# Attention layer and graph convolution on one core: the bias stores moved behind the row products, norms two rows at a time, one copy moved between engines, one start a unit later

## The chip, the cores and the metric

The kernel runs on one core of a Trainium2 chip. The metric is the device time of one execution in microseconds (us), the median of the runs shown. The core has five engines with a queue of instructions each: TensorE (PE in the profile) multiplies matrices, VectorE (DVE) and ScalarE (ACT) do elementwise work and can read PSUM, where products accumulate, GpSimd (POOL) does elementwise work on SBUF, and SyncE (SP) issues transfers. POOL issues transfers too.

## The reference

All is float32; x is 4096 x 512 and adj is 4096 x 4096. Layer 0 is an attention whose scores have adj added twice, with a residual and a norm; layer 1 is a graph convolution with a residual and a norm.

```python
def _layernorm(x, axis=-1, eps=1e-5):
    m = jnp.mean(x, axis=axis, keepdims=True)
    v = jnp.var(x, axis=axis, keepdims=True)
    return (x - m) / jnp.sqrt(v + eps)

# layer 0: _L0_gnn_ref(x, adj, adj, Wq, bq, Wk, bk, Wv, bv)
q = x @ Wq.T + bq
k = x @ Wk.T + bk
v = x @ Wv.T + bv
a = q @ k.T * scale + spatial_encoding + edge_encoding   # both are adj
attn = jax.nn.softmax(a, axis=-1)
x = _layernorm(x + attn @ v)

# layer 1
h = jax.nn.relu(adj @ (x @ W1) + b1)       # W1: 512 x 128
out = adj @ (h @ W2) + b2                  # W2: 128 x 512
x = _layernorm(x + out)
```

## The kernel before

**Groups and units.** The 4096 query rows are cut into 8 groups of 512. A group's scores are made in 16 units of two key tiles each. Score products, sums of probabilities times x ("P x", line 488) and most other large products are cut by a scheme of seven half-size products in place of eight, in the order 1, 2, 6, 7, 5, 4, 3 (`ORDER`). A unit has seven slots, and in each slot PE does one half of a score product (line 351) and DVE reads one (line 364).

**What runs beside the scores.** While PE makes the scores of group g+1, the probabilities of group g are finished: DVE subtracts the row maximum (`shift`, line 394), ACT takes the exponential (line 398), POOL adds the row sums (`sums`, line 407) and two combinations of quarters (`px_t2`, lines 434 and 435), DVE forms further combinations (`px_t34`, line 441, and `px_t1`, line 446), and PE multiplies by x. The table `PREP` gives the unit and the slots in which each of the 16 pairs of a group is prepared; group 0 has its own first two entries (`PREP_FIRST`) and the last group its own first seven (`PREP_LAST`). P x is done in blocks of key pairs (0-2, 2-4, 4-8, 8-12, 12-16), in each block the seven products, and `px_read` takes a finished product from PSUM into `ot`: in the first block the products 1, 6, 7 and 3 are copied by ACT (line 459), all others are added by DVE (line 461). The items of P x lie in a list that is worked off between the score products, at a rate that spreads it over the units given: for group 0 from the third unit after its scores on (`work[s1 + 2]`, 15 units), for later groups from the second on (16 units). In the last group there are no further scores: the row work of group 6 is followed by three times as much P x in each gap, and six products of the next stage (line 936) are mixed in.

**Row work.** When P x of a group is done, its rows are multiplied by Wv (`rows_out_fast`, line 602, for groups 0 to 5; `rows_out`, line 563, for 6 and 7), x is added, DVE takes mean and variance of each row tile of 128 rows (lines 536 and 538), POOL turns them into a factor and a shift in three small instructions (lines 544, 545, 547), and ACT applies them (`rows_norm`, line 551). This gives x1. `add_b2` then has POOL add the bias b2 (line 631) and issue the store of x1 + b2 to DRAM (line 633), to be read in the last stage only. The buffers of these sums (`xb`) come from the ring of eight (tag `sa`) into which SP loads the keys of the scores (lines 252 and 257). PE transposes x1 (`project`, line 639), ACT copies the result (line 641), PE multiplies it by W1 (`project2`, line 648) and DVE copies that (line 651). `row_items` is the list that sets the order; `w(n)` stands for n items of P x between two of its steps:

```python
        def norm(r):
            return [item(0, rows_norm, g, r), item(0, add_b2, g, r)]
```

So in the kernel before the sum and the store of a row stand directly behind its norm.

**Order.** Each engine works its instructions in the order in which the program emits them; the program emits them slot by slot. There is no other scheduler. The pool `form` of the first stage is closed at unit 18, and memory that it held is used again, among others by the first `ot` (`OT[0]`) and by the fourth buffer for x (`load_x(3)`, which waits in SP's queue). That memory is free once the store `u_d<-uo` of the first stage has been read out; POOL computes the last `uo` (line 206) and issues that store (line 196).

**After the groups** come the two products with adj (line 936 and the stages behind it) and the last norm.

Of the kernel before, what the change touches and what calls it, by code (L numbers as in the profile page):

```python
# [11 lines left out]
F32 = mybir.dt.float32  # L12
AF = mybir.ActivationFunctionType
ALU = mybir.AluOpType
# [4 lines left out]
P = 128  # L19
# [5 lines left out]
def tile_graph_attention_then_gcn(  # L25
# [51 lines left out]
    nc = tc.nc  # L77
# [4 lines left out]
    NG = N // W  # L82
    NP = NT // 2
# [14 lines left out]
    half_t = const.tile([P, 1], F32, name="half_t")  # L98
# [26 lines left out]
    small = att.enter_context(tc.tile_pool(name="small", bufs=4, side="right"))  # L125
# [30 lines left out]
    UT, UO, XTS, SA, S, XN, CB, MB, MACC, LACC, O, OT, RL, XR, T = ({} for _ in range(15))  # L156
# [293 lines left out]
    def px_read(g, first, k):  # L450

        letter = "PX" if k in (1, 6, 5, 3) else "PY"
        ps = T[letter].rearrange("p (f i) -> p f i", f=2)
        f, i = {1: (0, 0), 2: (0, 0), 6: (1, 0), 7: (1, 1), 5: (1, 1), 4: (1, 0), 3: (0, 1)}[k]
        to = OT[g][:, 2 * f : 2 * f + 2, ts(i, HW)]

        def go():
            if first and k in (1, 6, 7, 3):
                nc.scalar.copy(to, ps)  # L459
            else:  # L460
                nc.vector.tensor_tensor(to, ps, to, ALU.add)  # L461

        px_reads.append((letter, go))

    def read_px(letters=("PX", "PY")):
        for one in list(px_reads):
            if one[0] in letters:
                px_reads.remove(one)
                one[1]()
# [64 lines left out]
    def stats_of(pool, r):  # L534
        stats = pool.tile([P, nc.vector.BN_STATS_DIM], F32, tag="stats", name="stats")
        nc.vector.bn_stats(stats, r)
        mv = pool.tile([P, nc.vector.BN_AGGR_DIM], F32, tag="mv", name="mv")
        nc.vector.bn_aggr(mv, stats)
        return mv

    def norm_stats(pool, r, eps=EPS):
        mv = stats_of(pool, r)
        rstd = pool.tile([P, 1], F32, tag="rstd", name="rstd")
        nc.gpsimd.tensor_scalar(rstd, mv[:, 1:2], eps, None, ALU.add)
        nc.gpsimd.tensor_tensor(rstd, rstd, half_t, ALU.pow)
        shift = pool.tile([P, 1], F32, tag="shift", name="shift")
        nc.gpsimd.tensor_scalar(shift, mv[:, 0:1], rstd, -1.0, ALU.mult, ALU.mult)
        return shift, rstd

# [21 lines left out]
    def rows_out_fast(g, k, j):  # L571

        ot = OT[g].rearrange("p (f c) (h i) -> p f h c i", f=2, h=2)
        a11, a12, a21, a22 = (ot[:, f, h] for h in range(2) for f in range(2))
        tt = nc.vector.tensor_tensor

        def read(k):
            ps = T["VX" if k in (1, 6, 5, 3) else "VY"].rearrange("p (j o) -> p j o", j=2)  # L580
            h, i = QUARTER[k]
            to = XR[g][:, 2 * h : 2 * h + 2, ts(i, HW)]
            tt(to, ps, to, ALU.add)

        def stats(*rs):
            for r in rs:
                T["norm", g, r] = norm_stats(small, XR[g][:, r, :], RL[g][:, r : r + 1])

        if (k, j) == (1, 0):
            read_px()  # L590
            T["s3"] = rowp.tile([P, 2, HW], F32, tag="x1t", name=f"s3_{g}")
            tt(T["s3"], a11, a21, ALU.subtract)
            tt(a21, a21, a22, ALU.add)
        if j == 0 and k in (1, 2, 7):
            if k != 1 and m_tags[0] == T["v tag"]:
                m_tags.reverse()
            T["VX" if k == 1 else "VY"] = mbank(f"v{g}_{k}")
            if k == 1:
                T["v tag"] = m_tags[-1]
        lhs = {1: a11, 2: a12, 6: a11, 7: T["s3"], 5: a21, 4: a22, 3: a12}[k]  # L600
        for c in range(2):
            nc.tensor.matmul(  # L602
                T["VX" if k in (1, 6, 5, 3) else "VY"][:, ts(j, HW)],
                lhs[:, c, ts(j, P)],
                WV[OPERANDS[k][1]][:, c, :],
                start=k in (1, 2, 7) and j == 0 and c == 0,
                stop=c == 1,
                skip_group_check=True,
            )
        n = ORDER.index(k)  # L610
        if j == 0 and n:
            read(ORDER[n - 1])
            if k == 2:
                tt(a11, a21, a11, ALU.subtract)
            if k == 6:
                tt(a12, a12, a11, ALU.subtract)
            if k == 3:
                stats(2, 3)
        if (k, j) == (3, 1):
            T["last", g] = lambda: (read(3), stats(0, 1))  # L620

    def rows_last(g):
        T.pop(("last", g))()
# [29 lines left out]
    def row_items(g, between):  # L653

        def item(us, f, *args):
            return us, lambda: f(*args)

        def out(r):  # L660
            return [item(0.86, rows_out, g, r, c) for c in range(ND)]

        def norm(r):
            return [item(0, rows_norm, g, r), item(0, add_b2, g, r)]

        def pro(r):
            return [item(0.44, project, g, r)]

        def pro2(r):
            return [item(0.9, project2, g, r)]  # L670

        w = between
        if g in FAST_V:
            return [
                *(item(0.86, rows_out_fast, g, k, j) for k in ORDER for j in range(2)),
                *w(1), item(0, rows_last, g), *norm(2), *norm(3), *w(2), *pro(2), *w(2), *pro(3),
                *w(1), *norm(0), *w(1), *pro2(2), *norm(1), *w(2), *pro(0), *w(2), *pro2(3), *w(2),
                *pro(1), *w(2), *pro2(0), *w(4), *pro2(1),
            ]
        return [  # L680
            *out(0), *out(1), *norm(0), *out(2), *norm(1), *out(3), *norm(2), *w(2), *pro(0),
            *norm(3), *w(2), *pro(1), *w(2), *pro2(0), *w(2), *pro(2), *w(2), *pro2(1), *w(2),
            *pro(3), *w(2), *pro2(2), *w(4), *pro2(3),
        ]


    with tc.tile_pool(name="wqk", bufs=1) as wp:
# [52 lines left out]
        for w_t, w_n in ((wq_t, wq_n), (wk_t, wk_n)):  # L740
            for o in range(ND):
                ps = bank("o", f"psw{o}", 4)
# [7 lines left out]
        for a in range(ND):  # L750
            ps = bank("o", f"psm{a}", 4)
# [42 lines left out]
    work = {}  # L794
# [149 lines left out]
    def strassen(n, beside, done=()):  # L944
# [52 lines left out]
    PREP = [  # L997
        (1, LATE), (2, EARLY), (2, LATE), (3, MID), (4, EARLY), (4, LATE), (5, EARLY), (5, LATE),
        (6, MID), (7, MID), (8, EARLY), (8, LATE), (9, MID), (10, MID), (11, MID), (12, MID),
    ]  # L1000

    PREP_FIRST = [(1, (2, 3, 4)), (1, (4, 5, 6)), *PREP[2:]]
    PREP_LAST = [
        (1, (2, 2, 3)), (1, (3, 4, 4)), (1, (5, 6, 6)), (2, EARLY), (2, LATE), (3, LATE), (4, MID),
        *PREP[7:],
# [2 lines left out]
    for n in range(NG * NG * len(ORDER)):  # L1008
        (g, d), k = divmod(n // len(ORDER), NG), ORDER[n % len(ORDER)]
        if g:  # L1010
            unit, place = divmod(2 * (n - 5), len(ORDER))
            at(unit, place, load_s, g, d, k)

    for g in range(NG):
        s0 = g * NP
        s1 = s0 + NP
        if g:
            for n, k in enumerate(ORDER):
                at(s0 - 2 + (2 * n + 1) // 7, (2 * n + 1) % 7, load_operand, g, k)
            at(s0 - 2 - (g == 1), 1, add_c0, g)  # L1020
            at(s0 - 2 - (g == 1), 3, row_consts, g)
        for q in range(NP):
            d, j = divmod(q, 2)
            if (g or d) and j == 0:
                early = 2 + (g == 1 and d == 0)
                at(s0 + q - early, 4, begin_scores, g, d)
                at(s0 + q - early, 5, add_scores, g, d)
            for h in range(2):
                n = 1 + 3 * (2 * j + h) if d < NP // 2 - 1 else 2 * j + h
                at(s0 + 2 * d + 2 + n // 7, n % 7, new_max, g, q, h)  # L1030
            unit, (n0, n1, n2) = {0: PREP_FIRST, NG - 1: PREP_LAST}.get(g, PREP)[q]
            at(s1 + unit, n0, shift, g, q, 0)
            at(s1 + unit, n1, shift, g, q, 1)
            at(s1 + unit, n1, exps, g, q)
            at(s1 + unit, n2, sums, g, q)
            at(s1 + unit, n2, px_t2, g, q)
        at(s1, 5, turn_max, g)
        at(s1 + 1, 1, spread_max, g)
        if g < NG - 1:
            at(s1 + 13, 4, row_sums, g)  # L1040
        at(s1 + 14, 0, load_rows, g)
        at(s1 + 15, 0, add_bv, g)
        px = px_items(g)
        if g == NG - 1:
            for n, (u, k) in enumerate(spare):
                px.insert((8, 14, 20, 26, 90, 150)[n], (0.86, lambda u=u, k=k: product(u, k)))
        if g:
            px.reverse()
            by = 3 if g == NG - 1 else 1
            items = row_items(g - 1, lambda n: [px.pop() for _ in range(n * by)])  # L1050
            work[s1 + 1] = NP, items + px[::-1]
        else:
            work[s1 + 2] = NP - 1, px

    for n in range(3):
        at(NP + 1, 2 + n, load_x, n)
# [9 lines left out]
    for unit in range(last_unit):  # L1066
# [30 lines left out]
        for n in range(len(ORDER)):  # L1097
            run(unit, n)
            g, place = divmod(unit * len(ORDER) + n, NP * len(ORDER))
# [19 lines left out]
    g = NG - 1  # L1119
# [26 lines left out]
    hp, _, yp, rowp, small = pools  # L1146
# [144 lines left out]
```

## Time and profile before

| what | value |
|---|---|
| median of 3 runs | 2352.41 us (2351.85 to 2352.57) |
| the profiled execution's own time | 2352.5 us |
| its span in the trace | 2350.7 us |
| mean granted clock of PE | 0.996 |
| PE busy | 2303.9 us (98%) |
| DVE busy | 1626.5 us (69%) |
| POOL busy | 1013.6 us (43%) |
| ACT busy | 401.4 us (17%) |

The span runs from the first to the last instruction; the execution's time has 1.8 us more around it. The stages follow one another in the span: preparation and the scores of group 0 up to about 251 us, then one group in some 217 us, the last scores at 1745 us, P x of the last group to 1900 us, the products with adj from there to about 2265 us, and the tail. A busy share is a mean over these stages, so the views by window tell more than the totals.

### The profile page before, as it was taken

The numbers are of one execution on the slowest core, as the hardware profiler recorded it, in microseconds if no ns is written. First come the engines' busy times: TensorE is split into PE (matmuls) and PEld (weight loads), VectorE is DVE, ScalarE is ACT, GpSimd is POOL, SyncE is SP. The second block draws the span as 40 slices with busy tenths as digits, with TensorE's granted clock in tenths as the row PEclk, the third lists the DMA queues.
The fourth block names the chain that finished last, engine by engine and source line by source line (L and its number), as shares of the span: only waits on it lengthen the run. The fifth ranks groups of instructions, "written<-read, shape, count | busy, mean of one in ns | idle before, by whom it ended". The sixth has DMA issues, their size and how long they took to land.

```text
span 2350.7 us, 28200 instructions
## 1 busy us (share of the span) xinstructions
PE 2303.9 (98%) x10518; PEld 1726.2 (73%) x10518; DVE 1626.5 (69%) x2266; ACT 401.4 (17%) x421; POOL 1013.6 (43%) x1023
## 2 busy tenths in 40 slices
PE   9999999999999999999999999999998999999998
PEld 5666788878888888888888888888885843333456
DVE  4556476686668766866776686668656777888864
ACT  2111211131112112211311221121102100000012
POOL 1566464184327424641752284236428840011043
PEclk9999999999999999999999999999998999999999
DMA  5889787757758784777577577857663658999996
GB/s 159 268 274 312 217 226 204 206 159 200 217 152 212 198 237 118 206 201 224 147 207 214 159 199 199 227 129 218 185 198 100 205 205 313 334 348 370 352 383 223
DMA packets 276887, 523.28 MB, mean 223 GB/s; under 512 B 19152, under 2 KB 126416, under 8 KB 275856
## 3 DMA queue, kind: packets, MB, share of 16 engines
q1 hardware_dynamic: 229040, 406.12, 51.6%
q0 software_dynamic: 42176, 105.39, 20.5%
q10 hardware_dynamic: 5536, 9.97, 1.2%
q8 instruction: 84, 1.38, 0.2%
q14 instruction: 51, 0.42, 0.1%
HBM read 473.44 MB, written 46.40 MB: 221 GB/s over the span
## 4 chain that ended last, share of the span: by engine, by line
PE 85%; DVE 7%; POOL 4%; DMA 2%; issue 1%; ACT 0%; POOLq 0%; SPq 0%; DVEq 0%; ACTq 0%
PE p L488 29%; PE X L351 16%; PE b L936 15%; PE Y L351 12%; PE psu L171 4%; DVE s L394 3%; PE v L602 3%; PE acce L1236 2%; PE ops L1190 1%; DVE s L364 1%; POOL lacc L407 1%; DVE macc L373 1%; DVE s L441 1%; PE tps L648 1%; PE x L563 1%
## 5 line engine op out<-in xcount | busy, mean ns | idle before, releaser
L488 PE MATMUL p<-s,xn 128*128 128x256 f32 x3584 | 901.7, 381 | 24.9 <-ACT ot L459 6.9
L488 PEld LDWEIGHTS p<-s,xn 128*128 128x128 f32 x3584 | 678.7, 191 | 134.3 <-DVE s L446 8.7
L351 PE MATMUL X<-ut,sa 128*128 128x256 f32 x1984 | 514.1, 382 | 3.7 <-DVE s L364 3.7
L351 PEld LDWEIGHTS X<-ut,sa 128*128 128x128 f32 x1984 | 371.1, 190 | 88.1 <-issue 25.1
L407 POOL TENSOR_TENSOR lacc<-lacc,s 128x512 f32<-128x512 f32 x240 | 345.5, 1440 | 185.1 <-ACT s L398 175.3
L364 DVE TENSOR_TENSOR s<-X,s 128x512 f32<-128x512 f32 x256 | 176.3, 689 | 300.0 <-PE X L351 295.9
L351 PE MATMUL Y<-ut,sa 128*128 128x256 f32 x1408 | 361.1, 379 | 1.1 <-DMA sa<-in_xT_dram 1.1
L351 PEld LDWEIGHTS Y<-ut,sa 128*128 128x128 f32 x1408 | 266.4, 190 | 47.8 <-issue 12.9
L398 ACT ACTIVATE s<-s 128x1024 f32<-128x1024 f32 x128 | 135.4, 1058 | 805.4 <-DVE s L394 805.4
L295 POOL DMA_DIRECT2D s<-in_adjT_dram x64 | 84.0, 1312 | 404.8 <-ACT s L290 401.8
L373 DVE TENSOR_TENSOR macc<-macc,s 128x512 f32<-128x512 f32 x240 | 249.6, 1040 | 1.3
L364 DVE TENSOR_TENSOR s<-Y,s 128x512 f32<-128x512 f32 x192 | 132.1, 688 | 164.4 <-PE Y L351 163.7
L394 DVE TENSOR_TENSOR s<-s,mb 128x512 f32<-128x512 f32 x256 | 236.7, 934 | 3.3 <-ACT mb L321 3.3
L461 DVE TENSOR_TENSOR ot<-p,ot 128x512 f32<-128x512 f32 x248 | 169.3, 683 | 47.4 <-PE p L488 34.0
L903 DVE TENSOR_TENSOR tt<-ck 128x1024 f32<-128x1024 f32 x112 | 138.6, 1272 | 38.9 <-PE b L936 34.5
L936 PE MATMUL b<-tt,st 128*64 128x512 f32 (+1 forms) x768 | 156.1, 541 | 0.0
L441 DVE TENSOR_TENSOR s<-s 128x512 f32<-128x512 f32 x128 | 131.8, 1050 | 0.0
L171 PE MATMUL psu<-xt,m_t 128*128 128x512 f32 x256 | 128.0, 592 | 0.0
L434 POOL TENSOR_TENSOR s<-s 128x256 f32<-128x256 f32 x128 | 123.1, 962 | 0.6
L290 ACT COPY s<-cb 128x2048 f32<-128x2048 f32 x64 | 120.8, 1888 | 0.6
L936 PEld LDWEIGHTS b<-tt,st 128*64 128x64 f32 x768 | 53.9, 137 | 87.8 <-issue 79.9
L435 POOL TENSOR_TENSOR s<-s 128x256 f32<-128x256 f32 x128 | 108.6, 848 | 10.0
(159 smaller groups left out, 1987.0 us busy)
## 6 DMA issues: line engine op xcount, KB each, us to landing
ck<-in_adjT_dram SPq DMA_DIRECT2D x128, 1024.0 KB, 7.3
s<-in_adjT_dram POOLq DMA_DIRECT2D x64, 1024.0 KB, 11.2
sa<-s_d SPq DMA_DIRECT2D x224, 256.0 KB, 4.9
xn<-in_x_dram SPq DMA_DIRECT2D x192, 256.0 KB, 3.3
xn<-xs_d SPq DMA_DIRECT2D x96, 512.0 KB, 4.5
sa<-in_xT_dram SPq DMA_DIRECT2D x168, 256.0 KB, 4.5
xn<-xs_d SPq DMA_DIRECT2D x64, 256.0 KB, 3.7
u_d<-uo POOLq DMA_DIRECT2D x7, 1792.0 KB, 7.3
```

Source lines behind the costliest of these rows:

```text
L171: nc.tensor.matmul(ps[o], m_t[:, c, ts(o, P)], XTS[b][:, c, :], start=c == 0, stop=c == ND - 1)
L351: nc.tensor.matmul(T["X" if k in (1, 6, 5, 3) else "Y"][:, ts(j, HW)], SA[g, d, a][:, c, j, :], UT[g, b][:, c, :], start=k in (1, 2, 7) an ...
L364: nc.vector.tensor_tensor(ck, ps, ck, ALU.add)
L373: nc.vector.tensor_tensor(MACC[g], MACC[g], ck[:, h, :], ALU.max)
L394: nc.vector.tensor_tensor(ck, ck, MB[g], ALU.subtract)
L398: nc.scalar.activation(ck, ck, AF.Exp, scale=2.0)
L407: nc.gpsimd.tensor_tensor(LACC[g], LACC[g], ck[:, h, :], ALU.add)
L441: nc.vector.tensor_tensor(b, b, t2, ALU.subtract)
L461: nc.vector.tensor_tensor(to, ps, to, ALU.add)
L488: nc.tensor.matmul(T["PX" if k in (1, 6, 5, 3) else "PY"][:, ts(f, HW)], XN[n][:, q - a, ts(f, P)], quarters(g, q)[{1: 0, 2: 2, 6: 1, 7: 0 ...
L903: nc.vector.tensor_tensor(t[:, :2], v[:, :, 1], v[:, 0], ALU.subtract)
L936: nc.tensor.matmul(BK[n][k][ts(half, HH)], lhs, right(u, i, half, b), start=q == 0, stop=q == NP - 1,)
```

## The change

1. `px_read` in the last group (g = 7): the four copies of the first block (products 1, 6, 7, 3) are done by DVE and not by ACT.
2. In groups 0 to 5 the two rows of a pair (2 and 3, then 0 and 1) get their factor and shift together: four POOL instructions on two columns in place of twice three on one. Groups 6 and 7 keep one row at a time.
3. `add_b2` is taken out of `norm` and becomes items of its own (`b2`), which stand at the end of `row_items`, behind the last `project2`, with P x items between them. It holds for groups 0 to 6.
4. Group 0 uses `PREP` for all its pairs, and its P x list starts one unit later and is spread over 14 units, not 15.

```diff
         def go():
             if first and k in (1, 6, 7, 3):
-                nc.scalar.copy(to, ps)
+                if g == NG - 1:
+                    nc.vector.tensor_copy(to, ps)
+                else:
+                    nc.scalar.copy(to, ps)
             else:
                 nc.vector.tensor_tensor(to, ps, to, ALU.add)
...
-        def stats(*rs):
-            for r in rs:
-                T["norm", g, r] = norm_stats(small, XR[g][:, r, :], RL[g][:, r : r + 1])
+        def stats(r):
+
+            mv = small.tile([P, 4], F32, tag="mv", name="mv2").rearrange("p (n s) -> p n s", n=2)
+            for n in range(2):
+                st = small.tile([P, nc.vector.BN_STATS_DIM], F32, tag="stats", name="stats")
+                nc.vector.bn_stats(st, XR[g][:, r + n, :])
+                nc.vector.bn_aggr(mv[:, n], st)
+            rstd = small.tile([P, 2], F32, tag="rstd", name="rstd2")
+            tt = nc.gpsimd.tensor_tensor
+            tt(rstd, mv[:, :, 1], RL[g][:, r : r + 2], ALU.add)
+            tt(rstd, rstd, half_t.to_broadcast([P, 2]), ALU.pow)
+            sh = small.tile([P, 2], F32, tag="shift", name="shift2")
+            tt(sh, mv[:, :, 0], rstd, ALU.mult)
+            nc.gpsimd.tensor_scalar(sh, sh, -1.0, None, ALU.mult)
+            for n in range(2):
+                T["norm", g, r + n] = sh[:, n : n + 1], rstd[:, n : n + 1]
...
             if k == 3:
-                stats(2, 3)
+                stats(2)
         if (k, j) == (3, 1):
-            T["last", g] = lambda: (read(3), stats(0, 1))
+            T["last", g] = lambda: (read(3), stats(0))
...
         def norm(r):
-            return [item(0, rows_norm, g, r), item(0, add_b2, g, r)]
+            return [item(0, rows_norm, g, r)]
+
+        def b2(r):
+            return [item(0, add_b2, g, r)]
...
                 *w(1), *norm(0), *w(1), *pro2(2), *norm(1), *w(2), *pro(0), *w(2), *pro2(3), *w(2),
-                *pro(1), *w(2), *pro2(0), *w(4), *pro2(1),
+                *pro(1), *w(2), *pro2(0), *w(4), *pro2(1), *w(2), *b2(2), *w(4), *b2(3), *w(4), *b2(0),
+                *w(4), *b2(1),
             ]
         return [
             *out(0), *out(1), *norm(0), *out(2), *norm(1), *out(3), *norm(2), *w(2), *pro(0),
             *norm(3), *w(2), *pro(1), *w(2), *pro2(0), *w(2), *pro(2), *w(2), *pro2(1), *w(2),
-            *pro(3), *w(2), *pro2(2), *w(4), *pro2(3),
+            *pro(3), *w(2), *pro2(2), *w(4), *pro2(3), *w(2), *b2(0), *w(4), *b2(1), *w(4), *b2(2),
+            *w(4), *b2(3),
         ]
...
-    PREP_FIRST = [(1, (2, 3, 4)), (1, (4, 5, 6)), *PREP[2:]]
...
-            unit, (n0, n1, n2) = {0: PREP_FIRST, NG - 1: PREP_LAST}.get(g, PREP)[q]
+            unit, (n0, n1, n2) = (PREP_LAST if g == NG - 1 else PREP)[q]
...
-            work[s1 + 2] = NP - 1, px
+            work[s1 + 3] = NP - 2, px
```

`PREP` begins with `(1, (3, 5, 6)), (2, (1, 2, 4))`: unit, then the slots of the two shifts, and of the row sum. The tiles of the single-row norm get two or four columns in place of one or two, of which the same ones as before are used.

More of the change, by code (lines that the diff above doesn't have):

```diff
@@ L536, in stats_of @@
         nc.vector.bn_stats(stats, r)
-        mv = pool.tile([P, nc.vector.BN_AGGR_DIM], F32, tag="mv", name="mv")
+        mv = pool.tile([P, 4], F32, tag="mv", name="mv")[:, : nc.vector.BN_AGGR_DIM]
         nc.vector.bn_aggr(mv, stats)
@@ L542, in norm_stats @@
         mv = stats_of(pool, r)
-        rstd = pool.tile([P, 1], F32, tag="rstd", name="rstd")
+        rstd = pool.tile([P, 2], F32, tag="rstd", name="rstd")[:, :1]
         nc.gpsimd.tensor_scalar(rstd, mv[:, 1:2], eps, None, ALU.add)
         nc.gpsimd.tensor_tensor(rstd, rstd, half_t, ALU.pow)
-        shift = pool.tile([P, 1], F32, tag="shift", name="shift")
+        shift = pool.tile([P, 2], F32, tag="shift", name="shift")[:, :1]
         nc.gpsimd.tensor_scalar(shift, mv[:, 0:1], rstd, -1.0, ALU.mult, ALU.mult)
```

## The prediction

> **What bounds the kernel now.** The busy table of the page comes first, then PE's waits, then windows.
>
> ```profile
> ## 1 busy us (share of the span) xinstructions
> PE 2303.9 (98%) x10518; PEld 1726.2 (73%) x10518; DVE 1626.5 (69%) x2266; ACT 401.4 (17%) x421; POOL 1013.6 (43%) x1023
> ```
>
> PE is the bound, and the change neither adds nor removes a product. So it can only fill or open holes on PE, which are worth little: 46.8 us of the span without work, and some time at half clock. The view of PE's waits says where the holes are (who waited, for whom: us in total, times, longest):
>
> ```profile
> PE p L488 <- ACT ot L459: 6.9, 3, 4.4
> PE p L488 <- POOL xb L631: 6.7, 1, 6.7
> PE p L488 <- DVE s L446: 4.3, 3, 2.0
> PE x1ps L639 <- ACT xr L551: 3.3, 6, 0.6
> ```
>
> All four are waits of P x or of a row product on something that the change moves. The windows around the two large ones (busy time of PE, PEld, DVE, ACT, POOL, then granted clock):
>
> ```profile
> 262.00:268.00 6.00, 2.96 (x8) 2.40 (x9) 1.89 (x3) 3.44 (x3) 1.75 (x3) 0.78 0.62 203
> 1770.00:1800.00 30.00, 21.14 (x81) 13.89 (x81) 15.72 (x16) 8.87 (x12) 27.16 (x32) 0.77 0.24 72
> ```
>
> In the 30 us after 1770 PE idles 8.9 us, and the clock is 0.77, while POOL is full. The timelines of ACT and POOL there (start, length, engine, line, operation; in brackets the idle time before and its releaser) explain the hole:
>
> ```profile
> 1780.36 0.81 ACT L551 ACTIVATE xr<-xr,shift,rstd 128x512 f32<-128x512 f32 x1 [6.16 <-POOL shift L547]
> 1781.08 0.56 ACT L459 COPY ot<-p 128x512 f32<-128x512 f32 x1
> ```
>
> ```profile
> 1776.77 1.26 POOL L631 TENSOR_TENSOR xb<-xr,b_t 128x512 f32<-128x512 f32 x1
> 1778.33 0.67 POOL L633 DMA_DIRECT2D x_d<-xb  x1 [0.30 <-POOL xb L631]
> 1779.08 0.23 POOL L544 TENSOR_SCALAR rstd<-mv 128x1 f32<-128x1 f32 x1
> ...
> 1780.06 0.26 POOL L547 TENSOR_SCALAR shift<-mv,rstd 128x1 f32<-128x1 f32 x1
> ```
>
> Product 6 may start at 1781.74, once the copy (L459) has read product 1. The copy stands in ACT's queue behind the norm of row 2; the norm waits for a shift that POOL makes behind a row sum and the bias sum and store of row 0. The waits view names POOL for this hole; the link to PE is ACT's copy.
>
> Earlier, ACT's first `ot` copy sits on memory:
>
> ```profile
> 264.40 0.59 ACT L459 COPY ot<-p 128x512 f32<-128x512 f32 x1 [11.72 <-DMA u_d<-uo]
> ```
>
> **What the skill says, and the trace.** (1) The Trainium skill, "TensorE: Matmul & The Clock Gate", section "What's actually happening", has PE drop to half clock after an idle window of about 3.4 us and come back after as long at work. The trace agrees: behind the holes of 4.52 and 7.08 us P x products start every 0.43 us, not every 0.216; eight such cost 1.7 us. (2) The same page, section "Architectural detail: the array is 16× 32×32, not 1× 128×128", makes ACT's queue strict first in, first out; the copy behind the norm above agrees. (3) "VectorE: DVE Perf Modes", section "Why PSUM operands drop a tier", keeps float32 from PSUM at one element a cycle; the trace has such 128x512 DVE copies at 658 ns (L1244) to 692 ns (L717) against 565 to 599 ns for ACT's L459. I use 0.66. (4) "SBUF — State Buffer", section "SBUF: two separate sides", has POOL and two-input DVE instructions lock each other out of a shared port. The trace agrees in direction: DVE L446 on 128x256 takes 1.36 us at 500.98 beside POOL's sum, where two took 1.28 at 1787.09.
>
> **The change part by part**, as PE time. Stalls below are distances between starts of PE instructions less the back-to-back distance, so a little over the waits of the views.
>
> *Group 0 a unit later.* Before, P x starts at 254.48 and needs `ot` at 260.5; the memory comes free at 264.2 (store issued at 258.20 behind 5.5 us of POOL L206). Stall 4.52, then eight products at half clock, 1.7. After, unit 18 holds scores alone, seven slots of four products at 0.215 = 6.0 us, so the copy is due at about 266.7, and 264.2 + 0.59 = 264.8 is in time. The first row sum now follows the store in POOL's queue; the store's operands come from ACT at 252.7, so it is not earlier. The next adj load (L295) moves behind it to some 266 and lands by 276, read near 275.5 to 280: 0 to 1. SP's `load_x(3)`, stuck from 246.7 to 264.3 on the same store, is asked for one unit later behind loads that then run ahead. New: in unit 18 PE outruns the reads of DVE (0.69 each, shifts 0.7 beside): 0.1 to 0.8, as the 0.95 at 253.51. The remaining P x is denser by a fifteenth: nothing, as its rate is set by PE. Sum **-5.5**, range -8 (the 1.9 of small stalls at 294 to 303 go too) to -2.
>
> *b2 behind the rows, groups 0 to 5.* Four sums of 1.3 us and four issues of 0.6 (plus 0.3 of gap), 8.4 us of POOL per group, move from slots 487.8 to 500.8 (and the like) to about 20 us later. Beside them DVE was slow: L373 2.25 us at 498.21 (mean 1.04), L394 1.53, L446 1.36, and PE waited 2.17 at 502.40 and 0.52 at 505.64; group 2 has 0.84 at 938.39 and others 0.29. Their cover gone, POOL idles there. Gain 3.5 in group 0, 0.8 in group 2: -4.3. Who is behind the moved sums? Row sums and `px_t2` of pairs 5 to 7, four to eight us later. In group 1 pair 7 ends at 746.65 and PE reads it at 775.24: 28.6 of slack; pairs 4 to 6 have 31 to 40. Their cost: nothing, or +1 of new contention. The 0.81 and 0.74 at 736.96 and 742.09 of each group stay: DVE's reads, with POOL full in both kernels. SP: the ring slots of `xb` already hold it up 86.7 us in 12 waits and 28.4 in 6, and no score product of these groups waits for a load; spread out they hold it less at a time. -4.3 to +6.
>
> *Norm pairs.* Four small POOL instructions (0.28, 0.57, 0.28, 0.28 with gaps) before two shifts, in place of three before the first and six before the second. The second row gains, but row 2 and row 0 go first: row 2's shift waits for row 3's statistics (1.0 us) and comes at 697.9 for 697 (group 1), row 0's 0.3 later. PE waits 0.72 for row 0 (six times, 3.3 in the view); I add 0.3 each in six groups: **+1.5**, from 0 to +3. With b2: **-2**, range -5 to +8.
>
> *Last group.* Four copies go from ACT to DVE: +4 x 0.66 on DVE, which has 7.48 us idle at 1781.67 for want of that copy. POOL loses two bias sums and stores (4.2 us) ahead of row 2's shift and row 3's. New order at 1774.2: DVE copies product 1 (to 1774.9), adds product 2 (0.69), L441 twice (2.1 to 3.75), L394 1.2, L446 1.28: ends 1780.8 to 1783. PE, no longer held, wants product 7 of pair 0 at 1777.9, of pair 1 at 1778.9, product 5 at 1780.5: stalls of 1 to 4, say 2.4. They replace 7.08 + 2.33 and the half clock behind them, in all 14.9 from 1781 to 1798, of which 0.9 at the mixed-in products stays. **-11.6**, range -13.5 to -5. The four b2 of group 6 now lie between pairs 8 and 12, at 1810 to 1834. POOL idles 14.2 us from 1800 to 1860 and starts that stretch 8.4 earlier, against PE earlier by 11; slack of pairs 8 to 14 is 13.7 to 31.7. Pair 15 has 2.08, but the 4.55 us of idle before pair 14 (waiting for ACT) takes up lateness first. Cost nothing; if that cover were gone, up to 6.3.
>
> Sum: 5.5 + 2 + 11.6 = 19.1 off the profiled 2352.5 (0.1 over the median), so **2333.3**.
>
> **The rivals.** *A, DVE takes the place of ACT and POOL.* Its chain from 1774 on is the next to be late; at twice what I take per link beside a full POOL, PE idles past the clock window again and the part gives 5, not 11.6; and unit 18's reads or the adj load may take back 3.5 in group 0. For it: DVE instructions at 1.9 us each at 1782; against: 7.5 us of idle on DVE beforehand. Then 19.1 - 6.6 - 3.5 = 9: 2343.5.
> *B, slower: the late b2 hold ring slots.* SP's in-order loads of the keys wait for a slot until the store lands 2.7 us after issue; SP now reaches it while POOL still has full row sums from 727 to 755 ahead. If a group's loads come 6 us past need, 7 groups cost 42: 2352.5 - 19 + 42 = 2375. It decides from 19.1 / 7 = 2.7 us per group on. For it: waits of 12.8 to 14.2 us in SP's view already; against: these stall no product, and the slots are less bunched.
> *C, nothing: within 0.2% (4.7 us, about what a measurement of this kernel can tell from no change).* Group 0's and the last group's gains are half each (9) and the pairs and new contention at 1.2 per group take 7: 2350.
>
> **How the numbers follow.** Forecast 0.60, 2326 to 2339; A 0.21, 2339 to 2347; B 0.11; C 0.08. The forecast and A are faster (0.81), C the same, B slower. Range 2325 to 2347 holds the first two. Both large holes have one named cause that the emitted order takes away; the sizes of what is late next are the doubt.
>
> **What would show it.** Right: no wait of ACT's L459 on `u_d<-uo` above 1 us, and clock 1.00 from 262 to 274; the copy in the last group a DVE line that starts near 1768 (earlier by group 0), PE's busy time over the 30 us there up from 21.1 to 26 or more; the wait on L446 near 502 gone; that on L551 still there, some 5 in all. Wrong: a hole over 3.4 us in the last group behind L441 or L446 (A), score products waiting for `sa` (B), or P x waiting for L435 by more than a microsecond.

## The result and the profile after

| | before | changed |
|---|---|---|
| median | 2351.85 us (5 runs, 2349.74 to 2352.57) | 2328.71 us (5 runs, 2328.14 to 2332.29) |
| ratio to before, 95% interval | | 0.9905 (0.9891 to 0.9919) |
| the profiled execution's own time, span | 2352.5, 2350.7 | 2332.29, 2330.5 |

The change takes off 23.1 us, 1.0%; the forecast was 19.1 (2333.3). The profiled execution of the changed kernel is the slowest of its five, 3.6 over their median. One of twelve executions of the kernel "group 0 alone" below ran at a lower clock (2426.11 us) and is left out of its figures. The busy table:

```profile
PE 2298.2 (99%) x10518; PEld 1725.5 (74%) x10518; DVE 1615.2 (69%) x2270; ACT 399.1 (17%) x417; POOL 1004.8 (43%) x999
```

PE has the same 10518 products. DVE has four instructions more and is busy 11.3 us less. PE's waits, as before (who for whom: us in total, times, longest):

```profile
PE p L491 <- DVE s L441: 5.9, 6, 1.9
...
PE X L351 <- DVE s L364: 3.9, 5, 1.0
PE p L491 <- DVE s L446: 2.6, 2, 1.7
PE x1ps L655 <- ACT xr L554: 2.3, 6, 0.4
PE Y L351 <- DVE s L364: 1.8, 1, 1.8
PE x1ps L655 <- ACT x1t L657: 1.5, 1, 1.5
```

The two rows of 6.9 and 6.7 us at the head of the list are gone. What is left is mostly DVE. A third row of before that is gone is one that the prediction does not show; it becomes important below:

```profile
PE p L488 <- POOL s L435: 3.3, 5, 0.7
```

The windows (PE, PEld, DVE, ACT, POOL busy, granted clock) that answer to those of before:

```profile
262.00:268.00 6.00, 6.00 (x30) 5.28 (x29) 3.22 (x6) 1.18 (x2) 5.84 (x7) 1.00 0.46 159
268.00:274.00 6.00, 4.67 (x22) 3.80 (x21) 6.00 (x6) 1.53 (x2) 5.84 (x6) 1.00 1.09 250
1757.00:1787.00 30.00, 27.79 (x140) 20.25 (x139) 19.96 (x31) 9.05 (x12) 27.65 (x30) 1.00 0.27 79
```

In the last group PE does 27.8 us of work in the 30 us where it did 21.1, at full clock. Around 265 us the hole is closed too, but six microseconds later PE idles 1.3 us with DVE at 6.00 of 6.00. ACT's first copy shows that the memory was no longer in the way; it waits for the product itself:

```profile
265.70 0.59 ACT L462 COPY ot<-p 128x512 f32<-128x512 f32 x1 [3.11 <-PE p L491]
```

**Where the time went.** All kernels of this study emit PE's 10518 products in one order, but for those between 254 and 450 us, where a later start of group 0 mixes the same products (of one size, but for ten) in another way. So the start of the n-th product can be compared. The table has the change of the lead against the kernel before (us, negative is won) from one of eight points to the next, at 156.9, 272.9, 438.0, 546.7, 1644.4, 1799.0, 1839.8 and 2340.7 us of the kernel before. Each row is one profiled execution, of the changed kernel its slowest.

| kernel | group 0 to 273 | 273 to 438 | rows of group 0 | rows of groups 1-5 | last group to 1799 | to 1840 | rest |
|---|---|---|---|---|---|---|---|
| changed | -5.1 | +6.3 | -4.5 | -10.5 | -11.0 | +3.4 | +0.2 |
| b2 moved alone | 0.0 | 0.0 | -4.2 | -9.7 | -2.3 | +3.3 | +0.1 |
| changed, b2 put back | -5.2 | +4.6 | -0.3 | +8.7 | -6.5 | +1.0 | +0.2 |
| pairs alone | -0.3 | 0.0 | -0.4 | +8.6 | -0.7 | 0.0 | +0.1 |
| changed, no pairs | -4.9 | +4.6 | -4.2 | -9.7 | -11.1 | +3.4 | +0.1 |
| group 0 alone | -5.2 | +4.6 | -2.1 | 0.0 | -0.2 | 0.0 | 0.0 |
| changed, group 0 as before | -1.1 | 0.0 | -4.5 | -10.5 | -11.0 | +3.5 | 0.0 |
| before, sum left out | 0.0 | 0.0 | -3.5 | -7.1 | -1.9 | +0.1 | +0.1 |
| changed, b2 of group 6 later | -4.5 | +4.6 | -4.5 | -11.0 | -11.0 | +0.1 | +3.6 |
| the same, norms reordered | -5.0 | +4.6 | -4.5 | -10.6 | -13.7 | 0.0 | +3.8 |
| the same, b2 closer together | -5.0 | +4.6 | -4.5 | -11.1 | -13.7 | 0.0 | +3.9 |
| changed, PREP_FIRST kept | -7.3 | +4.4 | -4.5 | -11.1 | -11.0 | +3.4 | +0.1 |
| combined | -7.5 | +4.4 | -4.5 | -10.6 | -13.7 | 0.0 | +3.9 |

Seven tenths of the gain lie where the prediction saw little: in the rows of groups 0 to 5, 2 us in each of five groups and 4.5 in the first. One such place, on DVE's timeline of the kernel before (start, length, engine, line):

```profile
733.96 1.17 DVE L394 TENSOR_TENSOR s<-s,mb 128x512 f32<-128x512 f32 x1
735.05 1.21 DVE L373 TENSOR_TENSOR macc<-macc,s 128x512 f32<-128x512 f32 x1
...
737.38 1.24 DVE L394 TENSOR_TENSOR s<-s,mb 128x512 f32<-128x512 f32 x1
...
739.14 2.29 DVE L441 TENSOR_TENSOR s<-s 128x512 f32<-128x512 f32 x2
```

and the same instructions in the changed kernel (the read L464 stands between them in both):

```profile
730.53 0.67 DVE L394 TENSOR_TENSOR s<-s,mb 128x512 f32<-128x512 f32 x1
731.13 1.21 DVE L373 TENSOR_TENSOR macc<-macc,s 128x512 f32<-128x512 f32 x1
...
733.47 0.68 DVE L394 TENSOR_TENSOR s<-s,mb 128x512 f32<-128x512 f32 x1
734.07 0.68 DVE L464 TENSOR_TENSOR ot<-p,ot 128x512 f32<-128x512 f32 x1
734.67 1.28 DVE L441 TENSOR_TENSOR s<-s 128x512 f32<-128x512 f32 x2
```

Two of L394 and two of L441 took 0.5 us less each. In the changed kernel DVE has idle time (0.83 us before 736.78) and PE does not wait. In the kernel before PE was held up 0.81 and 0.74 us here. The second time it waited for DVE alone. The first time two engines were late together:

```profile
736.96 0.67 PE L488 MATMUL p<-s,xn 128*128 128x256 f32 x2 [0.65 <-POOL s L435]
```

This product needs a combination that POOL makes (`px_t2`); it ended at 736.84, and DVE's read of `ot` (L461), 0.02 us later at 736.86. It is so in each of groups 1 to 5: the combination ends 0.12 us before the product starts, the read 0.10 us. In the changed kernel the combination ends 1.25 us ahead of the same product. So the sums and stores of b2 had made POOL's own work late too, and not only slowed DVE.

### The profile page after: what moved, and what is told of

It reads as the page before. It is cut to its first block, busy times and chain, and to the rows that moved or that the text cites. A ratio compares the mean times of both kernels' runs of the same rounds, so it can differ in the third digit from the quotient of the medians.

```text
span 2330.5 us, 28148 instructions
## 1 busy us (share of the span) xinstructions
PE 2298.2 (99%) x10518; PEld 1725.5 (74%) x10518; DVE 1615.2 (69%) x2270; ACT 399.1 (17%) x417; POOL 1004.8 (43%) x999
## 4 chain that ended last, share of the span: by engine, by line
PE 91%; DVE 4%; POOL 2%; issue 1%; DMA 1%; ACT 0%; POOLq 0%; SPq 0%; DVEq 0%; ACTq 0%
PE p L491 31%; PE X L351 18%; PE b L957 14%; PE Y L351 13%; PE psu L171 4%; PE v L618 3%; PE acce L1256 2%; PE ops L1210 1%; PE tps L664 1%; PE x L566 1%; DVE s L441 1%; PE x1ps L655 1%; DVE s L364 1%; PE psm L774 1%; DVE s L446 1%
## 5 line engine op out<-in xcount | busy, mean ns | idle before, releaser
L364 DVE TENSOR_TENSOR s<-X,s 128x512 f32<-128x512 f32 x256 | 176.2, 688 | 292.4 <-PE X L351 288.4
L373 DVE TENSOR_TENSOR macc<-macc,s 128x512 f32<-128x512 f32 x240 | 254.2, 1059 | 1.2
L364 DVE TENSOR_TENSOR s<-Y,s 128x512 f32<-128x512 f32 x192 | 132.0, 688 | 174.9 <-PE Y L351 174.1
L394 DVE TENSOR_TENSOR s<-s,mb 128x512 f32<-128x512 f32 x256 | 232.1, 916 | 2.5 <-ACT mb L321 2.5
L464 DVE TENSOR_TENSOR ot<-p,ot 128x512 f32<-128x512 f32 x248 | 169.0, 681 | 30.4 <-PE p L491 30.0
L441 DVE TENSOR_TENSOR s<-s 128x512 f32<-128x512 f32 x128 | 126.4, 1010 | 0.0
L435 POOL TENSOR_TENSOR s<-s 128x256 f32<-128x256 f32 x128 | 107.1, 837 | 10.0
## 6 DMA issues: line engine op xcount, KB each, us to landing
s<-in_adjT_dram POOLq DMA_DIRECT2D x64, 1024.0 KB, 11.6
```

What stands on the lines that cost most here:

```text
L364: nc.vector.tensor_tensor(ck, ps, ck, ALU.add)
L373: nc.vector.tensor_tensor(MACC[g], MACC[g], ck[:, h, :], ALU.max)
L394: nc.vector.tensor_tensor(ck, ck, MB[g], ALU.subtract)
L441: nc.vector.tensor_tensor(b, b, t2, ALU.subtract)
```

## The experiments

Theory: POOL's sums over 512 columns stretch those DVE instructions that run beside them. What the move of b2 changes is which DVE instructions these are; where P x and DVE are in step, that costs PE, and elsewhere nothing. Rivals: the norms in pairs made the gain; POOL's queue time counts (it makes POOL's own combinations late), not what its sum does to DVE; group 0's later start gained something that only the one profile hides.

**b2 moved alone.** The kernel before with the edits of `norm`, `b2` and both lists of `row_items`.

> The kernel before with the b2 items moved behind the rows' products and nothing else. Theory (POOL's sums of b2 slowed DVE in the stretch where P x and the row work wait for DVE, in every group): the gain of groups 0 to 5 in the changed kernel's trace, 15 us between the ends of group 0's P x and of group 5's rows, comes back whole here, and the 7 us hole of the last group shrinks too, since row 2's shift no longer stands behind two sums: 2351.9 - 15 - 4 = 2333, between 2329 and 2338. Rival (the norms in pairs made that gain): at most 6 us less than before, 2346 or more.

Measured: 2340.31, ratio 0.9954 (0.9939 to 0.9968), so 11.6 less than before, and above the range that I expected. Groups 0 to 5 gain 13.9, as in the changed kernel (15.0); this part of the theory holds. The last group, where I expected 4, gains nothing in the end. ACT's timeline there says why:

```profile
1764.93 0.81 ACT L551 ACTIVATE xr<-xr,shift,rstd 128x512 f32<-128x512 f32 x1 [3.96 <-POOL shift L547]
1765.65 0.56 ACT L459 COPY ot<-p 128x512 f32<-128x512 f32 x1
```

The norm still waits for POOL (row sum and `px_t2` of one pair are ahead of it), and the copy still stands behind the norm. Two sums fewer make the hole shorter by 2.3 us, and the moved sums cost 3.3 later.

**b2 put back in the changed kernel.** The reverse edit.

> The changed kernel with the b2 items put back directly behind the norms; norm pairs, DVE copies and group 0's later start stay. Theory: groups 0 to 5 lose their 15 us again, and in the last group a part of the stall comes back, as the shifts wait behind the sums though the copy does not: 2328.7 + 15 + 2 = 2346, 2341 to 2350. Rival (pairs): 2335 or less.

Measured: 2356.01, ratio 1.0021 (1.0011 to 1.0030): 10 us more than expected, and slower than the kernel before. The last group behaves as expected (-5.5 from the copies alone), but groups 1 to 5 lose 8.7 where I expected nothing won or lost. Something else in the changed kernel costs 1.7 us a group as long as b2 is in its old place; the next experiment names it.

**Pairs alone.** The kernel before with the new `stats`.

> The kernel before with the norms of groups 0 to 5 two rows at a time, nothing else. Theory from the changed kernel without its move of b2, which lost 1.8 us in each of groups 1 to 5 against the kernel before, to waits for L364, L446 and the ot read: pairs shift the sums of b2 and the row sums of POOL onto other DVE instructions, and cost while b2 is there: 2352 + 5 x 1.8 = 2361, 2358 to 2363. Rival (that loss comes from group 0's later start or the copies): 2350 to 2354.

Measured: 2360.93, ratio 1.0042 (1.0027 to 1.0056). It is the pairs. PE's waits in this kernel:

```profile
PE p L488 <- DVE s L446: 11.5, 7, 1.7
PE X L351 <- DVE s L364: 8.6, 8, 1.1
...
PE p L488 <- DVE ot L461: 4.1, 7, 0.6
```

They were 4.3, 4.6 and 1.6. With two small POOL instructions fewer for each pair of rows, POOL's first sum of b2 starts at 704.79 in group 1 where it started at 707.49, while PE is only 1.3 us ahead there. The sums and row sums now fall on the DVE instructions that P x is waiting for: by this kernel's DVE timeline, L373 takes 1.65 us at 704.97, L394 1.75 at 707.14, and the two L441 1.67 and 1.56 from 709.41 on. In the kernel before these were 0.68, 0.68, 0.68 and 1.01. Less work on POOL made the kernel 10 us slower.

**No pairs in the changed kernel.** `stats` as before.

> The changed kernel with the norms of groups 0 to 5 one row at a time again. Theory: the trace of the move of b2 alone has 9.6 us won in groups 1 to 5 against 10.5 in the changed kernel, so pairs are worth about 1 us: 2329.7, 2327 to 2332. Rival (the prediction's +1.5 for pairs): 2327 or less.

Measured: 2331.17, ratio 0.9915 (0.9900 to 0.9930), against 0.9905 for the changed kernel; the intervals overlap. In the traces the pairs win about 1 us: the rows of groups 1 to 5 have -10.5 to -11.1 in the seven kernels that have both the pairs and b2 moved, and -9.7 in the two with b2 moved and no pairs. So pairs cost 8.6 with b2 in its old place and gain about 1 with b2 moved: the sign of one edit depends on the other.

**The sum left out, the store kept.** In the kernel before:

```diff
-        xb = sap.tile(...)
-        nc.gpsimd.tensor_tensor(xb, XR[g][:, r, :], b2_t, ALU.add)
-        nc.gpsimd.dma_start(x1_d[i // 2][:, i % 2], xb)
+        nc.gpsimd.dma_start(x1_d[i // 2][:, i % 2], XR[g][:, r, :])   # g < 7
```

> The kernel before, with the sum x1 + b2 of groups 0 to 6 left out: the store of x1 itself stays where it was, so b2 is missing from the output. POOL keeps the issue (0.6 us) and loses the sum (1.3 us), as does the ring the buffers. Theory (POOL's sum reads and writes SBUF beside DVE instructions with two SBUF inputs and stretches those): most of what the move gained in groups 0 to 5 is here too, 4 us at group 0's rows and 2 in each of five others: 2351.9 - 12 = 2340, 2336 to 2343. Rival (what counts is that POOL's queue is occupied, issue and all): the 1.3 of 2.2 us each leave half, 2346 or more.

Measured: 2340.98, ratio 0.9951 (0.9936 to 0.9966). Groups 0 to 5 win 10.6 of the 13.9 that the move won, without any moved instruction. That is the theory's figure, not the rival's. But a sum left out takes 1.3 us from POOL's queue as well, so this run does not part the two: the waits for POOL's combination (L435) are gone with it too. In groups 1 to 5 they are 0.81 of some 1.9 us a group, at the place where DVE was as late; how much either would cost alone is not shown. That a part belongs to the store's queue time, or to the ring buffers that go as well, is also left open. The hole of the last group stays here too (1.9 won), now behind POOL's row sum, the two combinations and the issue of a store.

**Group 0 alone, and the changed kernel without it.** The last part of the change (`PREP` for all pairs, P x a unit later) on the kernel before, and undone in the changed one.

> The kernel before with group 0's later start and PREP for all pairs, nothing else. Theory from the trace of the changed kernel, where 4.9 us are won by 273 us and given back by 308 us to waits for DVE's L441 and L364: no gain, 2352 within 3 us. Rival (my prediction's -5.5; the loss at 301 us is of the one profiled run): 2346.

> The changed kernel with group 0 as before (PREP_FIRST, P x from the third unit). Theory: the same as the changed kernel within 3 us, 2326 to 2332, with the 4.5 us wait of the first copy on u_d back and the waits on L441 near 274 and 301 us gone. Rival: 2334 or more.

Measured: 2349.49, ratio 0.9991 (0.9982 to 1.0000); and 2329.55, ratio 0.9906 (0.9891 to 0.9921), where the changed kernel has 0.9905. Alone, group 0's later start gains some 2 us (by the interval, 0 to 4), of which the trace has 2.1 at the rows of group 0, and beside the others nothing that can be measured. The table shows the reason in every row with it: 5 us won by 273 us and 4.6 (6.3 in the changed kernel's profile) given back by 438.

**PREP_FIRST kept with the later start.** In the changed kernel the two first pairs of group 0 are prepared early again.

> The changed kernel with group 0's P x a unit later, but PREP_FIRST kept (the first two pairs prepared early). Theory: the early pairs take the DVE work of the shifts and POOL's sums out of the unit where P x starts, so part of the waits for L441 and L364 at 273 to 301 us go and 1 to 3 us of the group 0 gain stay: 2326.5, 2325 to 2329. Rival (these waits come from the density of P x alone): the same as the changed kernel, 2328.7, or more.

Measured: 2329.87 (2326.32 to 2332.52), ratio 0.9908 (0.9894 to 0.9923). Its own profile has 2.2 us more of the early gain (-7.3 to 273 us, +4.4 after), as the theory says, and so has the combined kernel below (-7.5); the median does not show it. PE's wait of 1.96 us in the unit before P x starts, at 260.96 in the changed kernel, is not there. So it came from giving up the early pairs, not from the later start. What is given back, 4.4, hardly depends on the early pairs. Most of it is waits for DVE; that the denser P x makes DVE late is likely, but no run changes the density alone.

**b2 of group 6 later.** `w(2)` ahead of the first `b2` of the list for group 6 becomes `w(13)`: 33 P x items more.

> The changed kernel with group 6's four b2 items 33 P x items later, behind product 7 of block 4-8. Theory: the 3.3 us of waits for L441 and L446 between 1808 and 1816 of the changed kernel's trace are DVE slowed beside these sums; they go: 2328.7 - 3.3 = 2325.4, 2324 to 2327. Rival (P x is so dense there that DVE is late anyway, or the later sums slow DVE elsewhere): 2328 or more.

Measured: 2330.16, ratio 0.9909 (0.9892 to 0.9925): the rival. The 3.4 us between 1799 and 1840 are gone, and 3.6 appear behind 1840. In the changed kernel these were (POOL's sum, then DVE beside it and the row sum that follows):

```profile
1805.22 1.72 POOL L647 TENSOR_TENSOR xb<-xr,b_t 128x512 f32<-128x512 f32 x1
```

```profile
1805.73 3.95 DVE L441 TENSOR_TENSOR s<-s 128x512 f32<-128x512 f32 x2
```

Two L441 in 3.95 us, where two take 1.28 undisturbed. In the later version L441 and L446 of a later block are hit: there L446 takes 3.64 us for three at 1833.20.

**Norms reordered.** On top of that, in the list for group 6, `pro(0)` stands ahead of `norm(2)` and `pro(1)` ahead of `norm(3)`.

```diff
-            *out(0), *out(1), *norm(0), *out(2), *norm(1), *out(3), *norm(2), *w(2), *pro(0),
-            *norm(3), *w(2), *pro(1), *w(2), *pro2(0), ...
+            *out(0), *out(1), *norm(0), *out(2), *norm(1), *out(3), *w(2), *pro(0), *norm(2),
+            *w(2), *pro(1), *norm(3), *w(2), *pro2(0), ...
```

> As the kernel with group 6's b2 later, and its norms of rows 2 and 3 behind the transposes of rows 0 and 1, so that ACT's copy of a transpose does not stand behind a norm that waits for POOL. Theory: the waits of 0.90 and 1.64 us for ACT's copy at 1768 and 1774 go, about 2.5 us: 2323, 2321 to 2325. Rival (the transposes of rows 2 and 3 then wait for their norms, or L441 becomes the next in line): the same as without, 2325.

Measured: 2327.16, ratio 0.9897 (0.9882 to 0.9912), 3.0 under the kernel that it is built on (the intervals overlap); its trace wins 2.7 in the stretch to 1799. The size of the step is the one expected; the figure lies above the range because the kernel that it is built on did. The cause was the one that the changed kernel's ACT timeline shows:

```profile
1766.97 0.81 ACT L554 ACTIVATE xr<-xr,shift,rstd 128x512 f32<-128x512 f32 x1 [5.50 <-POOL shift L550]
1767.69 0.56 ACT L657 COPY x1t<-x1ps 128x512 f32<-128x512 f32 x1
```

The change had taken the `ot` copy from behind the norm; ACT's copy of the transpose still stood there.

**b2 of group 6 closer together.** `w(12)`, then `w(2)` between them.

> As the reordered kernel, with group 6's b2 items closer together (from 30 P x items later on, 6 apart), so that they end well before product 6 of block 8-12. Theory: the 2.6 us of waits for L441 and L446 at 1829 to 1837 go: 2327.2 - 2.6 = 2324.5, 2323 to 2326.5. Rival (the row sums behind them are late in any case, and POOL is full there): 2326.5 to 2328.

Measured: 2326.59, ratio 0.9901 (0.9886 to 0.9916). The figure is at the border between theory and rival; the trace is for the rival: 3.9 us are lost behind 1840, as with the looser spacing (3.8). POOL's row sums and the sums of the next stage follow without a gap, and in each of the three places that were tried for these four sums some block's L441 and L446 ran beside a full POOL.

**Combined.** The last kernel with PREP_FIRST kept.

> The tight kernel with PREP_FIRST kept: the changed kernel plus the two rearrangements of the last group's row work plus the early first pairs of group 0. If the pieces add up, 2326.6 in the tight kernel and 0 to 2.5 for the early pairs (their own profiled run was 2.3 ahead of the tight kernel's by 438 us, their median was not): 2325.5, 2323 to 2328, and 1.0% to 1.2% under the kernel before. If PREP_FIRST only adds spread, 2327 to 2330.

Measured: 2325.36 (2324.78 to 2329.43), ratio 0.9891 (0.9875 to 0.9908): the fastest median of all, 26.4 us under the kernel before and 3.4 under the changed one, whose interval it overlaps. Its waits on ACT's copies are gone, and DVE heads the list of what is left in the attention:

```profile
PE p L491 <- DVE s L441: 4.1, 4, 1.9
PE X L351 <- DVE s L364: 3.4, 5, 1.0
```

## Why the prediction was right, and where it was not

The forecast of 2333.3 lies 4.6 us above the median, inside the range. That the sum came so near is luck in part: two gains were forecast too large (group 0 and the last group, by some 5 and 4 us) and two too small (b2 by 9.6, the pairs by 2.5), and these nearly cancel.

- **Group 0, -5.5 forecast, +1.2 (the profiled execution) or -0.6 to +0.1 (six other profiles with the same edit) measured up to 438 us.** Four profiles of kernels that leave group 0 alone scatter from -1.1 to 0.0, so nothing was won. Up to 273 us the working held: copy due after the memory is free, no half clock, 5.1 won. Two steps failed. "0.1 to 0.8" for unit 18 was 1.96 at 260.96 us: DVE's read of a product came late behind L371 of 1.75 and L394 of 2.27 us, which ran beside POOL's combination of `uo` and the first row sum; with PREP_FIRST kept this wait is gone. And "the remaining P x is denser by a fifteenth: nothing, as its rate is set by PE" was wrong: PE waits for DVE 1.49 at 273.78, 0.99 at 277.47, 2.08 at 301.34, 1.15 at 334.68 and 0.80 at 387.57. The stall of before had given DVE 4.5 us to catch up.
- **b2 in groups 0 to 5, -4.3 forecast, -13.9 measured with the move alone.** Group 0's rows were near (3.5 forecast, 4.2 measured), though the waits listed for them, 2.17 and 0.52, make 2.7; a wait of 1.26 us for DVE at 510.45, which the list lacks, went too. The step that failed is "the 0.81 and 0.74 at 736.96 and 742.09 of each group stay: DVE's reads, with POOL full in both kernels". Both went, with the 0.29, in every group. By the timelines of group 1, POOL is about as full there in both kernels, but in the changed one the L394 and L441 that PE depends on fall beside the issues of the stores and their gaps, not beside row sums, and run at full speed. The reading itself was wrong for the larger one: the view has POOL's combination (L435) as its end, 3.3 us in five waits, with DVE's read 0.02 us behind it. And that the other was a read of DVE was no reason for it to stay: a read comes late when the instructions ahead of it in DVE's queue do. "Their cost: nothing" for the row sums behind them held.
- **Pairs, +1.5 forecast, about -1 measured.** I priced only the order of the shifts. Row 2's norm came later, as forecast: PE waits 0.37 for it, six times (2.3 in the view), where it had not waited. But the wait for row 0's norm, which I had growing by 0.3 each, went away (3.3 in the view of before). The larger effect, 8.6 us with b2 in its old place, is one I had not counted: POOL's sums moved by 1.4 us against PE, onto other DVE instructions.
- **Last group, -11.6 forecast, -7.6 measured.** The hole and its cause were right: 11.0 won by 1799, with DVE's chain quicker than assumed (two L441 in 2.30 us, and no wait for DVE in that chain). The stalls of 1 to 4 came from elsewhere: 2.5 us for ACT's copies of transposes behind the norms, which the prediction did not name. What failed is "cost nothing" for the four b2 of group 6: they cost 3.4. I had asked only whether `px_t2` would be late (it was not), and not what DVE does beside the sums.
- **Rivals.** A (DVE the next to be late) was right for group 0 and wrong for the last group up to 1799. B did not come: SP's waits for the store of `xb` fell from 115.1 us (86.7 and 28.4) to 44.4, and no score product waited for a load in these groups. C did not come.

What stays open, beside the shares of POOL and DVE in the gain of groups 1 to 5: why the same 2.08 us wait near 300 us is followed by half clock in the changed kernel's profile (0.72 in the window from 300 to 306 us, eight products at 0.43 to 0.49) and not in eight other profiles with the same wait. It is worth 2 us and may be part of the spread of these kernels, 2328 to 2332. The prediction took an idle time of 3.4 us as the condition for half clock; here 2.08 us was enough once.

## What to carry to other kernels

Before moving a POOL instruction, list the DVE instructions that will run beside it at the new place, and those that no longer do at the old one; and ask which of POOL's later instructions come earlier or later by it. When two engines end a wait within 0.02 us of each other, the view names one of them: look at both. When a stall is removed, engines that used it to catch up can be late next, so look at their busy share just behind the hole. And test edits that only shift an engine by a few microseconds together with those that they meet: here one edit cost 10 us alone and gained 1 beside another.

## What the runs showed of the hardware

Sorted by whether a POOL sum or difference of over 0.6 us overlaps them by more than 0.05 us, in the attention stage of the kernel before (250 to 1758 us), DVE's instructions fall into two kinds. Those with one operand in PSUM take the same time alone and beside POOL: L364 0.69 us in 220 and 166 cases, L461 0.68 in 145 and 72. Those with both operands in SBUF do not:

| line (before) | alone, median us (cases) | beside POOL, median us (cases), longest |
|---|---|---|
| L394, 128x512 | 0.68 (126) | 1.17 (95), 2.70 |
| L373, 128x512 | 0.68 (130) | 1.53 (80), 2.97 |
| L441, 128x512 | 0.68 (62) | 1.01 (50), 5.24 |
| L446, 128x256 | 0.41 (52) | 0.94 (60), 1.48 |

The Trainium skill, "SBUF — State Buffer", section "SBUF: two separate sides", says that only DVE instructions with two SBUF inputs (against a POOL instruction that reads SBUF), or in a two-port mode, contend with POOL; the trace agrees, and shows the size in this kernel, a factor of 1.5 to 2.3 in the median. I had used the statement for a direction only, and not for its second half: which of DVE's instructions are immune.
